# Graph attention in two layers: where each row's own logit terms lie, and which engine copies them out of PSUM

## The chip, the cores and the metric

The kernel runs on one core of a Trainium2 chip. A core has five engines that run beside each other[...]: PE (matrix products, which it writes to PSUM), DVE (vector operations), ACT (activations and copies), POOL (here it issues the indirect DMAs) and SP (here it issues the plain DMAs). Sixteen DMA engines move data between HBM and SBUF.

The metric is the device time in microseconds (us); the median of three runs counts. A time of this kernel is compared with another by that median. Inside one execution, the profile gives the start and length of every instruction.

## The reference

Eight graphs share one adjacency matrix of 2048 nodes (a node is its own neighbour too). Layer 0 is attention with one head on 256 features, layer 1 has four heads of 64. Cut to what matters:

```python
# layer 0: logits between node n and its neighbours m
e = leaky_relu((x @ W1) @ (x @ W2).T, 0.2)      # masked by adj
x = layernorm(x + relu(softmax(e) @ (x @ W3)))

# layer 1: four heads, D = 64
q = (x @ W).reshape(B, N, H, D)
e_src = einsum("bnhd,d->bnh", q, a[:D])          # a row's own term
e_dst = einsum("bnhd,d->bnh", q, a[D:])          # a neighbour's term
e = leaky_relu(e_src[:, :, None, :] + e_dst[:, None, :, :], 0.2)   # masked by adj
x = layernorm(x + elu(einsum("bijh,bjhd->bihd", softmax(e), q)))
```

Both terms are linear in x. So a row's q, its e_dst and its e_src come out of one product of x with a matrix of 256 + 4 + 4 columns. The neighbours need q and e_dst; only the row itself needs e_src.

## The kernel before

**Tiles and units.** The nodes are sorted by their number of neighbours and cut into 16 tiles of 128 rows (one row a partition). The eight graphs are two halves of four (HB = 4). A Unit is one layer, one half and one tile; there are 64, first the 32 of layer 0, then the 32 of layer 1. SLOTS gives each tile its number of neighbour slots, 12 to 38, 301 over all tiles.

**The ring.** For two slots at a time (CHUNK) POOL issues gathers of the neighbours' rows into one of 16 ring buffers (chunk_job, gather, L191). In layer 0 DVE multiplies each gathered row with the unit's vector g and sums it to a logit (logits0, L543), DVE and ACT make the softmax (L556 to L569), ACT weights the rows in place (sums0, L634), and PE sums them over the slots by products with an identity (add_slot, L612). Then the buffer is free for the next gather. In layer 1 DVE adds the own term to the gathered neighbour term (logits1, L747), most of the weighting is DVE's (L813), some of it ACT's (L809).

**The end of a unit of layer 0** is after0, and it is there that the change lies. The sum is transposed (L405, copied out of PSUM by ACT at L407), multiplied by W3 (projected, L415), added to the residual xr (L672), normalised (statistics, factors, normalise, L372 to L395) and stored to x1s (L687). Then y is transposed to x1T, and for each graph i of the half, with r, j = divmod(i, 2), two products of 264 columns (L696) go to one PSUM tile pq: 256 columns of q, 4 of e_dst, 4 of e_src. ACT copies the first 260 to qrow (L704); DVE copies the last 4 to the tile so (L705). Two DMAs on SP write so to the table own_d in HBM (L707, 32-byte pieces), and 8 steps later POOL scatters qrow to the table qg that layer 1 gathers from (store, L199).

qrow has one buffer, so two buffers, and the pool ps, from which pq comes, four banks for all products but the sums.

**Who reads own_d.** before1 loads the own terms of a unit of layer 1 as a whole row of 16 numbers (L728); logits1 adds them.

**What sets the order.** After the setup only POOL's order is the written one (manual_schedule with Pool). The instructions of PE, DVE, ACT and SP are put in an order for each engine when the program is built. In the code, tick advances at each slot the logits of coming units (stream), the starts of units (before0, before1), the end of the last unit (finish, after0) and the neighbour lists (neighbours, L491 to L500) by a step or two each. Every engine works through its own queue in order, so an instruction that waits holds all that stand behind it.

SP's queue carries in turn, for each unit of layer 0: four loads of xr (L512), the store of x1 (L687), the two stores of own terms (L707), later also the loads L728 and L787.

**The weights.** Weights.products computes the small columns: it multiplies W by a, and reduces over the 64 features of a head (L110) into wqs[:, k, 256:264].

Of the kernel before, what the change touches and what calls it, by code (L numbers as in the profile page):

```python
# [11 lines left out]
F32 = mybir.dt.float32  # L12
# [10 lines left out]
P = 128  # L23
ALPHA = 0.2
EPS = 1e-5
H = 4
# [21 lines left out]
class Weights:  # L48


    def __init__(self, nc, const, tmp, ps_tile, w1, w2, w3, wq, a, C, tag):
        KC = C // P
        self.ident = const.tile([P, P], F32, tag="ident", name=f"{tag}ident")
        make_identity(nc, self.ident)
        self.mhalf = const.tile([P, 1], F32, tag="mhalf", name=f"{tag}mhalf")
        nc.gpsimd.memset(self.mhalf, -0.5)
        self.roots = const.tile([P, 2], F32, tag="roots", name=f"{tag}roots")
        nc.gpsimd.memset(self.roots[:, 0:1], EPS)
        nc.gpsimd.memset(self.roots[:, 1:2], -math.log(2.0) / 3.0)
        self.w3 = const.tile([P, KC, C], F32, tag="w3", name=f"{tag}w3_sb")  # L60

        self.wqs = const.tile([P, KC, C + 2 * H], F32, tag="wqs", name=f"{tag}wqs")
        self.A = const.tile([P, KC, C], F32, tag="A", name=f"{tag}A")
        a_bc = const.tile([P, 2 * D], F32, tag="a_bc", name=f"{tag}a_bc")
        w12 = tmp.tile([P, 2, KC, C], F32, tag="t", name=f"{tag}w12")
        for t, src in ((w12[:, 0], w1), (w12[:, 1], w2), (self.w3, w3)):
            nc.scalar.dma_start(t, src.rearrange("(k p) d -> p k d", p=P))
        nc.scalar.dma_start(self.wqs[:, :, :C], wq.rearrange("(k p) d -> p k d", p=P))
        nc.scalar.dma_start(a_bc, a.rearrange("(o d) -> o d", o=1).to_broadcast([P, 2 * D]))

        self.given = w12, a_bc
        self.of = nc, tmp, ps_tile, C, tag

    def products(self):
        nc, tmp, ps_tile, C, tag = self.of
        w12, a_bc = self.given
        KC = C // P
        wT = tmp.tile([P, 2, KC, C], F32, tag="t", name=f"{tag}wT")

        for i in range(2):  # L80
            pt = ps_tile(f"{tag}ps_w{i}")
            ptv = pt[:, : KC * C].rearrange("p (k d) -> p k d", k=KC)
            for kd in range(KC):
                for kc in range(KC):
                    nc.tensor.transpose(
                        ptv[:, kd, ts(kc, P)], w12[:, i, kc, ts(kd, P)], self.ident
                    )
            nc.vector.tensor_copy(wT[:, i], ptv)
        pa = ps_tile(f"{tag}ps_A")
        for kc in range(KC):  # L90
            for kd in range(KC):
                nc.tensor.matmul(
                    pa[:, ts(kc, C)],
                    lhsT=wT[:, 0, kd, ts(kc, P)],
                    rhs=wT[:, 1, kd, :],
                    start=(kd == 0),
                    stop=(kd == KC - 1),
                )
        nc.vector.tensor_copy(self.A, pa[:, : KC * C].rearrange("p (k d) -> p k d", k=KC))

        for k in range(KC):
            for j in range(2):
                prod = tmp.tile([P, H, D], F32, tag="t", name=f"{tag}wa_{k}_{j}")
                nc.vector.tensor_tensor(
                    prod,
                    self.wqs[:, k, :C].rearrange("p (h d) -> p h d", h=H),
                    a_bc[:, ts(j, D)].unsqueeze(1).to_broadcast([P, H, D]),
                    ALU.mult,
                )
                nc.vector.tensor_reduce(  # L110
                    self.wqs[:, k, C + (1 - j) * H : C + (2 - j) * H], prod, AX.X, ALU.add
                )

    def rows_of(self, nc, const, j, C):

        self.wd = const.tile([P, C // P, P], F32, tag="wd", name="wd")
        nc.gpsimd.memset(self.wd, 0.0)
        for k in range(C // P):
            nc.vector.tensor_copy(
                self.wd[:, k, :].rearrange("p (h r) -> p h r", h=H)[:, :, 0],  # L120
                self.wqs[:, k, C + (1 - j) * H : C + (2 - j) * H],
            )
# [3 lines left out]
def fast_path(  # L126
# [24 lines left out]
    nc = tc.nc  # L151
    B, N, C = x.shape
    NT = N // P
    KC = C // P
    HB = B // 2
    HC = HB * C
    HG = HB * H
    HW = HC // 2
    CD = C + H
    QW = 2 * CD  # L160
# [3 lines left out]
    const = ctx.enter_context(tc.tile_pool(name="const", bufs=1))  # L164
# [5 lines left out]
    qp = ctx.enter_context(tc.tile_pool(name="q", bufs=1))  # L170
    hsp = ctx.enter_context(tc.tile_pool(name="hs", bufs=2))
    ep = ctx.enter_context(tc.tile_pool(name="e", bufs=3))
    sp = ctx.enter_context(tc.tile_pool(name="small", bufs=4))
# [9 lines left out]
    def ring_tile(name):  # L183
        return ring.tile([P, CHUNK * 2 * QW], F32, tag="ring", name=name)

    def wide_tile(name):
        return wp.tile([P, 2 * QW], F32, tag="t", name=name)
# [23 lines left out]
    own_d = [tc.dram_tile([N, HG], F32, name=f"own_{h}") for h in range(2)]  # L211
# [6 lines left out]
    w = Weights(nc, const, wp, ps_tile, w1, w2, w3, wq, a, C, "")  # L218
# [4 lines left out]
    for it in range(NT):  # L223
        r = ring_tile(f"adj_{it}")
# [99 lines left out]
    for r in range(2):  # L324
        rr = slice(64 * r, 64 * r + 64)
        pr = ps_tile(f"ps_half_{r}")[:, :NT]
        for c in range(2):
# [3 lines left out]
                rhs=ranked[rr, 0, :],  # L331
# [35 lines left out]
    def statistics(y, name):  # L367

        st = sp.tile([P, HB, nc.vector.BN_STATS_DIM], F32, tag="st", name=f"st_{name}", bufs=2)
        mv = sp.tile([P, HB, nc.vector.BN_AGGR_DIM], F32, tag="mv", name=f"mv_{name}")  # L370
        for b in range(HB):
            nc.vector.bn_stats(st[:, b, :], y[:, b, :])  # L372
            nc.vector.bn_aggr(mv[:, b, :], st[:, b, :])  # L373
            if b % 2 == 1:
                yield
        return mv
# [23 lines left out]
    def transposed(src, name, dst):  # L400

        for i in range(2):
            pt = ps_tile(f"ps_t_{name}_{i}")
            for j in range(4):
                nc.tensor.transpose(pt[:, ts(j, P)], src[:, ts(4 * i + j, P)], ident)  # L405
            yield
            nc.scalar.copy(dst[:, ts(i, 512)], pt)  # L407
        yield
# [253 lines left out]
    def after0(u):  # L662
        h, t, n = u.h, u.t, u.name
        while evictions:
            evictions.popleft()()
        hs = u.hs
        hT = wide_tile(f"hT_{n}")
        yield from transposed(hs, f"h_{n}", hT)
        y = wide_tile(f"y0_{n}")[:, :HC]

        def residual(i, pp):
            nc.vector.scalar_tensor_tensor(  # L672
                y[:, ts(i, 512)], pp, 0.0, u.xr[:, i, :], ALU.max, ALU.add
            )

        yield from projected(hT, w.w3, f"h_{n}", residual)
        yb = y.rearrange("p (b c) -> p b c", b=HB)
        mv = yield from statistics(yb, n)
        yield
        yield  # L680
        rstd, nmr = factors(mv, n)
        yield
        for b in range(HB):
            normalise(yb, yb, b, rstd, nmr)
            if b % 2 == 1:
                yield
        nc.sync.dma_start(x1s[h][ts(t, P), :], y)  # L687
        x1T = wide_tile(f"x1T_{n}")
        yield from transposed(y, f"x1_{n}", x1T)
        qrow = qp.tile([P, 2, QW], F32, tag="q", name=f"q_{n}")  # L690
        so = sp.tile([P, 2, HG // 2], F32, tag="so", name=f"so_{n}", bufs=2)
        for i in range(HB):
            r, j = divmod(i, 2)
            pq = ps_tile(f"ps_q_{n}_{i}")
            for k in range(KC):
                nc.tensor.matmul(  # L696
                    pq[:, : C + 2 * H],
                    lhsT=x1T[:, ts(i * KC + k, P)],
                    rhs=w.wqs[:, k, :],
                    start=(k == 0),  # L700
                    stop=(k == KC - 1),
                )
            yield
            nc.scalar.copy(qrow[:, r, ts(j, CD)], pq[:, :CD])  # L704
            nc.vector.tensor_copy(so[:, r, ts(j, H)], pq[:, CD : CD + H])  # L705
        for c in range(2):
            nc.sync.dma_start(  # L707
                own_d[h][ts(t, P), ts(c, HG // 2)].rearrange("(r p) g -> p r g", r=2),
                so[64 * c : 64 * c + 64],
            )  # L710

        def store():
            for r in range(2):
                scatter(
                    f"q{h}",
                    qg[h].rearrange("n (q c) -> (n q) c", q=2),
                    orderP[:, t, r : r + 1],
                    qrow[:, r, :],
                )
            tabled[0] += 1  # L720

        late.append((clock[0] + 8, store))


# [166 lines left out]
    for j, u in enumerate(units):  # L891
# [3 lines left out]
        elif j + 2 < NT:  # L895
            t = up[j + 2]
# [49 lines left out]
    for j, u in enumerate(units):  # L946
# [5 lines left out]
        if 2 <= j < 10:  # L952
            b, half = divmod(j - 2, 2)
            n = ts(half, N // 2)
# [311 lines left out]
```

## Time and profile before

| | |
|---|---|
| median of three runs | 2865.22 us (2856.55 to 2866.15) |
| the profiled execution | 2741.96 us, span from first to last instruction 2740.1 us |
| granted TensorE clock, mean | 0.842 |
| DMA | 749.51 MB, mean 274 GB/s |
| own-term stores (L707) | 64 issues of 4 KB, 1.8 us to landing, 615 ns of SP each |
| own-term copies (L705) | 128, first at 253.0 us, last at 1763.1 us |
| layer 0's logits (L543) | first at 136.6 us, last at 1683.4 us |
| layer 1's logits (L747) | first at 1686.3 us, last at 2687.6 us |

The span has three parts: the setup, whose last steps (the neighbour lists) run on beside layer 0; layer 0 until some 1780 us; and layer 1, which overlaps with the end of layer 0's last unit for some 100 us. In what follows a line of groups gives line, engine, operation, tiles and shapes, count | busy us and mean ns of one | the idle time of the engine just before them and what ended it. A line of waits gives who waited for whom, the sum in us, how often, and the longest. A line of the timeline gives the start in us, the length, the instruction and, in brackets, the idle time before it.

### The profile page before, as it was taken

What the parts mean: (1) busy time and instruction counts of PE and PEld (TensorE: products, weight loads), DVE (VectorE), ACT (ScalarE), POOL (GpSimd) and SP (SyncE); (2) the same over time, 40 slices, a digit from 0 to 9 for tenths busy, and PEclk for the clock granted to TensorE, in tenths of its full rate; (3) what the DMA queues carried; (4) which work ended last, traced back from release to release, by engine and by line L of the source; (5) the groups of instructions that cost most, each with busy time, mean ns of one, the idle gap of its engine ahead of it and who ended that gap; (6) DMA issues with size and microseconds to landing.
All of it is one profiled execution on the core that took longest, in us unless ns stands there. A gap on an engine that the chain in (4) does not pass through costs nothing. (4 is left out here: it accounts for less than half of the span.)

```text
span 2740.1 us, 42566 instructions
## 1 busy us (share of the span) xinstructions
PE 1857.8 (68%) x12003; PEld 792.3 (29%) x12003; DVE 2270.1 (83%) x7247; ACT 1827.9 (67%) x4937; POOL 1515.4 (55%) x1506
## 2 busy tenths in 40 slices
PE   0148888888786866686878767756656667655763
PEld 0124434333332333343434323312221222211221
DVE  7679999999987876777787786788888888888996
ACT  6137787878879986867878779644445555554454
POOL 1353454545444544544454545577767777777773
PEclk9569999999988988898988888877877878877876
DMA  9996776777765566767686774899789998997892
GB/s 388 380 376 207 270 262 245 260 245 263 261 221 200 183 215 215 252 212 268 219 277 217 242 263 154 287 332 357 268 315 354 348 344 317 358 351 269 305 354 89
DMA packets 248036, 749.51 MB, mean 274 GB/s; under 512 B 55712, under 2 KB 73248, under 8 KB 241648
## 3 DMA queue, kind: packets, MB, share of 16 engines
q0 software_dynamic: 192064, 644.32, 66.5%
q1 hardware_dynamic: 54464, 101.21, 10.4%
q8 instruction: 98, 1.61, 0.2%
q10 hardware_dynamic: 1264, 1.18, 0.1%
q14 instruction: 146, 1.20, 0.1%
HBM read 721.50 MB, written 84.48 MB: 294 GB/s over the span
## 5 line engine op out<-in xcount | busy, mean ns | idle before, releaser
L612 PE MATMUL acc<-s,ident 64*64 64x512 f32 x9632 | 1336.4, 653 | 469.0 <-issue 285.4
L543 DVE CUSTOM_DVE_ANT_0 j<-s,g 128x256 bf16<-128x256 f32 x2408 | 1019.9, 424 | 199.1 <-DMA s<-xg,idx 133.0
L191 POOL DMA_INDIRECT s<-xg,idx x602 | 632.4, 1051 | 771.7 <-ACT s L634 280.9
L634 ACT ACTIVATE s<-s,e 128x256 f32<-128x256 f32 x2408 | 1000.1, 506 | 28.3 <-DVE e L569 27.4
L191 POOL DMA_INDIRECT s<-qg,idx x602 | 614.8, 1021 | 233.4 <-issue 123.7
L612 PEld LDWEIGHTS acc<-s,ident 64*64 64x64 f32 x9632 | 391.1, 144 | 1211.5 <-issue 777.6
L813 DVE TENSOR_TENSOR s<-s,p 128x2048 f32<-128x2048 f32 (+1 forms) x262 | 577.5, 2222 | 0.0
L809 ACT ACTIVATE s<-s,e 128x64 f32<-128x64 f32 x1472 | 357.8, 335 | 47.1 <-DVE e L777 35.8
L543 DVE DVE_READ_ACCUMULATOR2_ANT e<- 128x1 f32 x2408 | 197.0, 82 | 0.0
L696 PE MATMUL ps_q<-wqs,x1T 128*128 128x264 f32 x512 | 147.7, 426 | 35.9 <-ACT x1T L407 25.1
L199 POOL DMA_INDIRECT out_dram<-o,oidx x128 | 130.2, 1017 | 71.5 <-ACT o L395 36.7
L405 PE MATMUL ps_t_x<-ident,xo 128*128 128x128 f32 x256 | 56.7, 365 | 162.7 <-DMA xo<-xg,order 162.6
L383 ACT ACTIVATE z<-mv,roots 128x4 f32<-128x4 f32 x64 | 19.0, 297 | 212.2 <-DVE mv L373 212.1
L747 DVE TENSOR_TENSOR e<-s,own 128x32 f32<-128x32 f32 (+1 forms) x312 | 56.9, 186 | 104.0 <-DMA s<-qg,idx 97.6
L415 PE MATMUL ps_p_g<-A,xT 128*128 128x256 f32 x512 | 129.4, 399 | 8.9 <-DVE so L705 5.2
L415 PE MATMUL ps_p_h<-w_sb,hT 128*128 128x256 f32 x512 | 127.8, 392 | 1.4 <-ACT hT L407 1.4
L696 PEld LDWEIGHTS ps_q<-wqs,x1T 128*128 128x128 f32 x512 | 100.8, 206 | 88.4 <-ACT x1T L407 32.8
L395 ACT ACTIVATE o<-xr,nmr,rstd 128x256 f32<-128x256 f32 x128 | 66.3, 589 | 76.9 <-DVE nmr L391 67.3
L415 PEld LDWEIGHTS ps_p_g<-A,xT 128*128 128x128 f32 x512 | 96.7, 196 | 53.2 <-ACT s L634 8.1
L763 ACT ACTIVATE e<-e 128x304 f32<-128x304 f32 (+11 forms) x34 | 14.9, 439 | 143.7 <-DVE e L762 143.7
L491 DVE MAX8 m<-nb 128x8 f32<-128x2048 f32 x44 | 100.5, 2286 | 11.9 <-DMA nb<-edges,order 11.7
L415 PEld LDWEIGHTS ps_p_h<-w_sb,hT 128*128 128x128 f32 x512 | 92.0, 189 | 63.3 <-issue 17.9
(130 smaller groups left out, 1486.2 us busy)
## 6 DMA issues: line engine op xcount, KB each, us to landing
adj<-in_adj_dram SPq DMA_DIRECT2D x16, 1024.0 KB, 8.9
edges<-adj SPq DMA_DIRECT2D x16, 1024.0 KB, 19.8
xr<-xo SPq DMA_DIRECT2D x128, 128.0 KB, 6.9
x1s<-y SPq DMA_DIRECT2D x32, 512.0 KB, 7.3
xr<-x1s SPq DMA_DIRECT2D x32, 512.0 KB, 6.9
s<-xg,idx POOLq DMA_INDIRECT x602
s<-qg,idx POOLq DMA_INDIRECT x602
xg<-in_x_dram SPq DMA_DIRECT2D x4, 2048.0 KB
```

The costliest lines, as they stand in the source:

```text
L191: nc.gpsimd.indirect_dma_start(out=dst, out_offset=None, in_=table, in_offset=AT(ap=index, axis=0), bounds_check=table.shape[0] - 1, oob_i ...
L199: ins = nc.gpsimd.indirect_dma_start(out=table, out_offset=AT(ap=index, axis=0), in_=src, in_offset=None)
L395: nc.scalar.activation(dst[:, b, :], y[:, b, :], AF.Identity, bias=nmr[:, b : b + 1], scale=rstd[:, b : b + 1],)
L415: nc.tensor.matmul(pp[:, ts(j, C)], lhsT=srcT[:, ts((2 * i + j) * KC + k, P)], rhs=weight[:, k, :], start=(k == 0), stop=(k == KC - 1),)
L491: nc.vector.max(m[:, ts(i, 8)], v)
L543: nc.vector.tensor_tensor_reduce(out=jt, in0=rows[:, s, ts(b, C)], in1=u.g[:, ts(b, C)], scale=1.0, scalar=0.0, op0=ALU.mult, op1=ALU.add, ...
L612: nc.tensor.matmul(acc[r][64 * c : 64 * c + 64, :], lhsT=ident[rr, rr], rhs=rows[rr, s, c * 2 * w_ : (c + 1) * 2 * w_].rearrange("p (j w) ...
L634: nc.scalar.activation(v, v, AF.Copy, scale=u.p[i][:, b, k : k + 1])
L696: nc.tensor.matmul(pq[:, : C + 2 * H], lhsT=x1T[:, ts(i * KC + k, P)], rhs=w.wqs[:, k, :], start=(k == 0), stop=(k == KC - 1),)
L747: nc.vector.tensor_tensor(e[:, c * CHUNK : c * CHUNK + ns, :].rearrange("p s (b g) -> p s b g", b=HB), rows[:, :ns, :].rearrange("p s (b w ...
L809: nc.scalar.activation(v[:, a, g, :], v[:, a, g, :], AF.Copy, scale=pv[:, a, g : g + 1])
L813: nc.vector.tensor_tensor(v, v, pv.unsqueeze(3).to_broadcast([P, n * HB, H, D]), ALU.mult)
```

## The change

The matrix of the small products gets four more columns, in front: sqs is [e_src | W | e_dst | e_src], and wqs is a view of its last 264 columns, so that all other users of wqs see what they saw. The four new columns are a copy of the last four.

For the first graph of a pair (j = 0) the product takes the columns from the front: own term, q, neighbour term. For the second (j = 1) it starts four columns later: q, neighbour term, own term. Side by side in qrow this gives own term, q, neighbour term, q, neighbour term, own term: the own terms lie at both ends, and what lies between is the table row of 520 numbers as before. ACT copies all 264 columns of pq, DVE none. The tile so is gone. The own terms are stored from qrow, by four DMAs of 16-byte pieces instead of two of 32-byte pieces, and the scatter takes the 520 numbers from between.

```diff
-        self.wqs = const.tile([P, KC, C + 2 * H], F32, tag="wqs", name=f"{tag}wqs")
+        self.sqs = const.tile([P, KC, C + 3 * H], F32, tag="wqs", name=f"{tag}wqs")
+        self.wqs = self.sqs[:, :, H:]
...
+            nc.vector.tensor_copy(self.sqs[:, k, :H], self.wqs[:, k, C + H :])
...
-        qrow = qp.tile([P, 2, QW], F32, tag="q", name=f"q_{n}")
-        so = sp.tile([P, 2, HG // 2], F32, tag="so", name=f"so_{n}", bufs=2)
+
+        qrow = qp.tile([P, 2, QW + 2 * H], F32, tag="q", name=f"q_{n}")
...
-                    rhs=w.wqs[:, k, :],
+                    rhs=w.sqs[:, k, j * H : j * H + CD + H],
...
-            nc.scalar.copy(qrow[:, r, ts(j, CD)], pq[:, :CD])
-            nc.vector.tensor_copy(so[:, r, ts(j, H)], pq[:, CD : CD + H])
+            nc.scalar.copy(qrow[:, r, ts(j, CD + H)], pq[:, : CD + H])
         for c in range(2):
-            nc.sync.dma_start(
-                own_d[h][ts(t, P), ts(c, HG // 2)].rearrange("(r p) g -> p r g", r=2),
-                so[64 * c : 64 * c + 64],
-            )
+            for j in range(2):
+                nc.sync.dma_start(
+                    own_d[h][ts(t, P), ts(2 * c + j, H)].rearrange("(r p) g -> p r g", r=2),
+                    qrow[64 * c : 64 * c + 64, :, j * (QW + H) : j * (QW + H) + H],
+                )
...
-                    qrow[:, r, :],
+                    qrow[:, r, H : H + QW],
```

Here C = 256, H = 4, CD = C + H = 260, QW = 2 * CD = 520, HG = 16.

## The prediction

> **What bounds the kernel now.** I read the page's busy shares and slices first, then the groups of the two instructions that the change touches.
>
> ```profile
> PE 1857.8 (68%) x12003; PEld 792.3 (29%) x12003; DVE 2270.1 (83%) x7247; ACT 1827.9 (67%) x4937; POOL 1515.4 (55%) x1506
> DVE  7679999999987876777787786788888888888996
> ACT  6137787878879986867878779644445555554454
> ...
> L704 ACT COPY q<-ps_q 128x260 f32<-128x260 f32 x128 | 47.0, 372 | 20.1 <-PE ps_q L696 20.1
> L705 DVE COPY so<-ps_q 128x4 f32<-128x4 f32 x128 | 20.0, 156 | 38.4 <-ACT q L704 38.3
> ```
>
> DVE is the busiest engine, but a slice is 68.5 us and the two layers differ, so I cut the span into stages. Columns are the stretch, its length, busy time of PE, PEld, DVE, ACT and POOL with counts, the granted clock, the DMA share and GB/s:
>
> ```profile
> 205.00:760.00 555.00, 462.99 (x2480) 210.27 (x2480) 533.84 (x2136) 434.41 (x1068) 261.30 (x249) 0.93 0.72 249
> 760.00:1780.00 1020.00, 764.37 (x4762) 355.88 (x4758) 776.99 (x3549) 822.31 (x2068) 491.20 (x472) 0.86 0.68 229
> 1780.00:2740.00 960.00, 583.45 (x4574) 199.25 (x4566) 816.92 (x1282) 492.45 (x1689) 692.02 (x677) 0.80 0.85 312
> ```
>
> Until about 760 us DVE is 96% busy (533.84 of 555): it is the bound there, because the neighbour lists are built on it beside the logits. From 760 to the end of layer 0 no engine is full. ACT leads with 81% (822.31 of 1020), and the work goes round a ring of 16 buffers: gather, DVE logits, ACT weighting, PE sum, next gather. From about 1780 layer 1 alone runs; the last copy of the changed line starts at 1763.1, so that part can only shift. The waits of 760 to 1715, DVE's and then ACT's (sum, count, longest):
>
> ```profile
> DVE j L543 <- DMA s<-xg,idx: 130.8, 86, 7.2
> DVE so L705 <- ACT q L704: 36.0, 24, 5.4
> ...
> ACT e L563 <- DVE e L562: 52.8, 17, 8.0
> ACT z L383 <- DVE mv L373: 29.8, 10, 8.1
> ACT s L634 <- DVE e L569: 12.5, 13, 1.6
> ACT y L395 <- DVE nmr L391: 11.1, 10, 3.2
> ```
>
> So the copy that moves matters by its wait, not its length. DVE stops for it 26 times in the run, 38.3 us, all after 760. The chain that ended last shows only the final scatters and decides nothing.
>
> The last view is DVE's instructions in order of time around a copy, one in the full stretch and one in the later stretch:
>
> ```profile
> 516.32 0.42 DVE L543 CUSTOM_DVE_ANT_0 j<-s,g 128x256 bf16<-128x256 f32 x1
> 516.66 0.09 DVE L543 DVE_READ_ACCUMULATOR2_ANT e<- 128x1 f32 x1
> 516.66 0.16 DVE L705 COPY so<-ps_q 128x4 f32<-128x4 f32 x1
> 516.78 0.42 DVE L543 CUSTOM_DVE_ANT_0 j<-s,g 128x256 bf16<-128x256 f32 x1
> 517.13 0.08 DVE L543 DVE_READ_ACCUMULATOR2_ANT e<- 128x1 f32 x1
> 517.25 0.42 DVE L543 CUSTOM_DVE_ANT_0 j<-s,g 128x256 bf16<-128x256 f32 x1
> ...
> 1303.93 0.16 DVE L705 COPY so<-ps_q 128x4 f32<-128x4 f32 x1 [1.49 <-ACT q L704]
> 1307.16 0.42 DVE L543 CUSTOM_DVE_ANT_0 j<-s,g 128x256 bf16<-128x256 f32 x1 [0.86 <-DMA s<-xg,idx]
> 1320.23 0.43 DVE L543 CUSTOM_DVE_ANT_0 j<-s,g 128x256 bf16<-128x256 f32 x1 [5.53 <-DMA s<-xg,idx]
> ```
>
> Two products with the copy between them start 0.46 us apart (516.32, 516.78); the next two, with none between, start 0.47 us apart (516.78, 517.25). The copy sits in the gap that the accumulator read leaves. And the 1.49 us lost at 1303.93 is followed by waits of 0.86 and 5.53 us for gathers.
>
> **What the Trainium skill says.** "PSUM — Partial Sum Buffer", section "PSUM bank collisions raise a hardware error": two engines must not touch one bank at once, two readers included, so they are ordered by semaphores. The trace agrees: the DVE copy starts after the ACT copy of the same bank, and 26 times DVE arrives early and waits. "VectorE: DVE Perf Modes", "The DRAIN you can't avoid": the next operation waits until the pipeline is empty, though one that is not held starts earlier. Here the measurement decides: the 0.16 us copy adds nothing between two products. "DMA: Bandwidth & Descriptors", "Specifications": transfers under 512 B are below line rate; this bears on the stores of 16 B pieces, of which the trace of before has only 32 B ones.
>
> **The change part by part.**
>
> *DVE copies removed.* 128 x 156 ns = 20.0 us of busy time. In the full stretch they ride in gaps as shown, so I count 0 to 2 us of path for the 45 copies before 760 (24 to 480, 21 to 760) and nothing for the later 83, since DVE has idle time there.
>
> *DVE's wait on ACT removed.* At most 38.3 us. What is late next, by place: at 1697.33 to 1705.33 four waits, 5.44 + 2.39 + 2.50 + 2.39 = 12.7 us, stand in the turn to layer 1, where ACT works through the last weights of layer 0 without a pause and the next exponential (1708.38) is queued behind them; worth 0. At 928.75 and 934.08, 4.7 us; ACT has no idle time from 915 to 965, so worth 0. The remaining 20.9 us are mostly followed within some 15 us by a gather wait of about the same or greater length, as at 1303.93; they pay only where DVE's lead reaches the end of a unit, where ACT waits for it. Upper reading of that: ACT waits for DVE 52.8 + 29.8 + 12.5 + 11.1 = 106.2 us from 760 to 1715; DVE itself waits 130.8 + 36.0 + 17.9 (its other five entries) = 184.7 us there, of which the copy's wait is 19.5%; 19.5% of 106.2 is 20.7 us. Lower reading: 3 us. I take the middle, 12 us.
>
> *PSUM banks freed by ACT's copy instead of DVE's.* PE waits for DVE's copy 5.7 us (L696) and 5.2 us (L415), before 760, where PE is 85% busy and DVE full. Between 0 and 10.9; I take 3.
>
> *ACT's copy grows from 260 to 264 columns.* 128x512 copies take 580 ns at L523 and 128x260 ones 372, so 208 / 252 = 0.83 ns a column; 4 columns x 128 copies = 0.4 us. On ACT, and hidden except where ACT is full.
>
> *Matmuls.* Still 264 columns (L696, 426 ns each), only from a window that starts 4 columns later for every second batch: 0.
>
> *SP's stores.* Four of 16 B pieces for each unit instead of two of 32 B: 64 more issues x 615 ns = 39 us of SP, 1.2 us a unit. What stands behind them on SP: the four residual loads (L512), then the x1 store (L687) and later own loads (L728). At 1013.23 the stores issue (1.28 us for two) and the next entry is at 1024.49, so two more delay nothing; and the loads are used a unit or more later. Without that cover it would be 1.2 x 32 = 38 us of lateness on SP. As to the DMA engines, the present stores land in 1.8 us (median); two times as many pieces I bound between 0 and 1 us of gather delay a unit, 0 to 32 us, and take 0, since the DMA share of layer 0 is 0.68 to 0.72 and the four are issued 0.6 us apart.
>
> *qrow's single buffer* is now read by these stores besides the two scatters. Before, it is free once the scatters land, about 20 us after the stores (stores 937.02, scatters 955.80 and 957.24), and the next unit's copies start at 1009.69, some 50 us later; the stores are not the last to let go. 0. Extra semaphore steps on ACT: 38 ns each, up to three a unit, 0 to 4 us; I take 0, in time ACT would have waited.
>
> *Setup.* Two DVE copies of 128x4, 0.3 us.
>
> *Order.* Only POOL's order is written out; the other queues are ordered when the program is built. In the code a q copy stands after one slot's four weightings, in the trace six of them stand between copies (931.01, 933.67), so the order is not the code's, and it may move with the DVE copies gone. Unseen; I bound it at 30 us either way and take 0.
>
> Sum: 12 + 3 - 0.3 = about 15 us. Against the profiled execution (2741.96 us, span 2740.1) this gives 2727. The runs' median, 2865.22, lies 4.5% above that execution, for which the page has no cause; I take the 15 us off unscaled: **2850 us**, -0.5%.
>
> **Rivals.**
> 1. *The wait is hidden anyway.* The gather waits take every freed microsecond: 3 us, 2862. For it: 1303.93, the two places where ACT is full, and the 130.8 us of gather waits beside 36.0. Against it: ACT does wait 106 us for DVE.
> 2. *The order turns against it* (slower). PE works in order and stands 132.5 us from 760 to 1715 at the transposes of xo (L405), 16 waits of 8.3 us each, because that gather lands late. While PE stands, no ring buffer is freed. If the new order puts those transposes about 1.5 us earlier against their gather in each of 32 units, that is 48 us, less the 15: 2898; it decides from 0.5 us a unit (16 us). A milder shift gives 2880. For it: the waits are long already and hang on the order alone. Against it: nothing in the change pushes them one way.
> 3. *The change doesn't do what it says*: DVE waits for ACT at another instruction (L566, L385) for the same reason. Same time as rival 1, and included there.
>
> **How the numbers follow.** About 0.5%, 14 us, is what a measurement can tell from no change. The forecast, with 15 us or more gained (2825 to 2851), 0.50; rivals 1 and 3, 0.25; rival 2, 0.25. A lucky order would carry the forecast to 2820. The range goes from 2818 to 2888, which leaves out the far end of rival 2 and an upper gain beyond 47 us. Faster 0.50, same 0.25, slower 0.25.
>
> **What would show it.** Right: no L705, DVE's gather waits grow by less than 25 us, ACT's waits on DVE fall below 90 us, PE's waits on so vanish, layer 0 ends some 15 us sooner and layer 1 keeps its length. Rival 1: gather waits up by 30 us or more. Rival 2: PE's wait on xo well above 162.6 us in total. The forecast fails if layer 1 changes its length by more than layer 0 does, or if ACT begins to wait for DMAs before its copy.

## The result, and the profile after

The changed kernel takes 2857.53 us (median of 20 runs, 2847.68 to 2862.42), the kernel before 2864.71 us on the same chip (20 runs). The ratio is 0.9975, with a 95% interval from 0.9967 to 0.9984: 7 us faster, between 5 and 10. The direction is the one forecast; the gain is just under half of the 15 us.

A warning ahead of all comparisons: the profiled execution after takes 2856.72 us, that of before took 2741.96. The change did not add 115 us. By all signs the two were taken on chips of different speed (the last section), so traces of after are compared here with an execution of the unchanged kernel on a chip where it takes 2865.09 us.

The page after, busy shares and DVE's slices; then the copy in the view of groups:

```profile
PE 2098.3 (73%) x12003; PEld 913.0 (32%) x12003; DVE 2268.4 (79%) x7121; ACT 1837.8 (64%) x4937; POOL 1511.6 (53%) x1506
DVE  7678999998988876777886866787777778877886
```

```profile
L706 ACT COPY q<-ps_q 128x264 f32<-128x264 f32 x128 | 47.5, 373 | 13.7 <-PE ps_q L698 13.5 <-PE ps_p_g L417 0.2
```

The first slices of DVE are as full as before (9 from slice 5 on); the later ones are lower, because layer 1 does the same work in more time on this chip. DVE has 126 instructions fewer (7247 to 7121: 128 copies gone, two in the setup added), and ACT's copy is as long as before (373 ns against 372). Code lines below L62 have moved down by one or two, so L543 is L545 now, and L704 is L706. The stages:

```profile
205.00:760.00 555.00, 454.68 (x2414) 208.65 (x2416) 517.48 (x2019) 427.86 (x1052) 253.41 (x242) 0.91 0.71 243
760.00:1780.00 1020.00, 776.20 (x4643) 359.79 (x4637) 769.94 (x3503) 818.38 (x2044) 484.39 (x465) 0.86 0.68 227
```

DVE is still the fullest engine until 760 us (517.48 of 555), ACT from then on. The waits of 760 to 1715, first DVE's, then ACT's:

```profile
DVE j L545 <- DMA s<-xg,idx: 129.3, 76, 6.9
DVE j L545 <- DVE e L545: 17.4, 29, 1.0
```

```profile
ACT e L565 <- DVE e L564: 57.3, 14, 11.5
ACT z L385 <- DVE mv L375: 16.4, 6, 7.7
ACT s L636 <- DVE e L571: 8.8, 9, 1.4
```

DVE's wait on ACT's copy is gone. In the unchanged kernel on a chip of this speed the same window shows:

```profile
DVE j L543 <- DMA s<-xg,idx: 112.4, 66, 7.3
DVE so L705 <- ACT q L704: 22.7, 20, 2.9
```

So 22.7 us of one wait went, and the gather wait grew by 16.9 (129.3 against 112.4). That already looks more like the first rival than like the forecast. Layer 1 kept its length: its logits run from 1701.9 to 2802.3 us after, from 1708.8 to 2811.1 in the unchanged kernel on the chip of that speed. Both are some 1101 us, so in these two traces most of the gain, 6.9 us, lies in layer 0. Of that, only 2.3 us had come when the 900th of DVE's 2408 products with gathered rows started (counted in the traces: 752.2 us against 754.5); the rest came later.

### The profile page after: what moved, and what is told of

Read it like the earlier page. It is cut to its first block, busy times and chain, and to the rows that moved or that the text cites. A ratio compares the mean times of both kernels' runs of the same rounds, so it can differ in the third digit from the quotient of the medians.

```text
span 2854.9 us, 42520 instructions
## 1 busy us (share of the span) xinstructions
PE 2098.3 (73%) x12003; PEld 913.0 (32%) x12003; DVE 2268.4 (79%) x7121; ACT 1837.8 (64%) x4937; POOL 1511.6 (53%) x1506
## 4 chain that ended last, share of the span: by engine, by line
PE 28%; DVE 23%; issue 19%; DMA 14%; ACT 8%; POOL 6%; another core or an unknown queue 1%; POOLq 0%; DVEq 0%; ACTq 0%; SPq 0%
PE acc L614 21%; DVE j L545 11%; ACT s L636 6%; DMA s<-xg,idx 4%; POOL s L193 4%; DMA xo<-xg,order 4%; DMA s<-qg,idx 3%; DVE s L815 2%; DVE m L493 2%; PE ps_p_g L417 2%; PE ps_p_h L417 2%; DVE e L545 2%; PE ps_q L698 1%; PE ps_t_x L407 1%
## 5 line engine op out<-in xcount | busy, mean ns | idle before, releaser
L614 PE MATMUL acc<-s,ident 64*64 64x512 f32 x9632 | 1572.3, 667 | 352.1 <-issue 209.7
L545 DVE CUSTOM_DVE_ANT_0 j<-s,g 128x256 bf16<-128x256 f32 x2408 | 1019.7, 423 | 239.7 <-DMA s<-xg,idx 129.8
L614 PEld LDWEIGHTS acc<-s,ident 64*64 64x64 f32 x9632 | 507.4, 146 | 1210.2 <-issue 941.5
L811 ACT ACTIVATE s<-s,e 128x64 f32<-128x64 f32 x1472 | 364.0, 336 | 82.7 <-issue 35.3
L545 DVE DVE_READ_ACCUMULATOR2_ANT e<- 128x1 f32 x2408 | 196.0, 81 | 0.0
L407 PE MATMUL ps_t_x<-ident,xo 128*128 128x128 f32 x256 | 56.3, 362 | 138.9 <-DMA xo<-xg,order 132.1
L493 DVE MAX8 m<-nb 128x8 f32<-128x2048 f32 x44 | 100.4, 2284 | 10.4 <-DMA nb<-edges,order 10.3
```

Of the source, the lines that this page charges most:

```text
L493: nc.vector.max(m[:, ts(i, 8)], v)
L545: nc.vector.tensor_tensor_reduce(out=jt, in0=rows[:, s, ts(b, C)], in1=u.g[:, ts(b, C)], scale=1.0, scalar=0.0, op0=ALU.mult, op1=ALU.add, ...
L614: nc.tensor.matmul(acc[r][64 * c : 64 * c + 64, :], lhsT=ident[rr, rr], rhs=rows[rr, s, c * 2 * w_ : (c + 1) * 2 * w_].rearrange("p (j w) ...
L811: nc.scalar.activation(v[:, a, g, :], v[:, a, g, :], AF.Copy, scale=pv[:, a, g : g + 1])
```

## The experiments

Three batches were run, each on one chip, and each kernel is compared with the kernel before on that chip. Where a kernel copies something that nothing uses, this is said.

### First batch: is it the wait or the bank?

**The kernel before, unchanged.**

> The kernel before, unchanged, for a profile whose span is near the median of its runs (the profiled execution of before was 4.3% shorter than that) and for the noise. Every theory expects a ratio of 1.000 within 0.001. If the profile is again near 2740 us, the profiled execution is what differs; near 2860, the layer 1 part is the one that is longer.

Measured: 2865.59 us, ratio 1.0004 (0.9994 to 1.0013). This is what no change looks like, and its trace is the reference above.

**The wait put back, without the bank.** DVE copies the own terms out of qrow once ACT has written them. The copy is unused. DVE waits for ACT as before, but PSUM is read by ACT alone.

```diff
             nc.scalar.copy(qrow[:, r, ts(j, CD + H)], pq[:, : CD + H])
+            own = j * (CD + H) + j * CD
+            nc.vector.tensor_copy(so[:, r, ts(j, H)], qrow[:, r, own : own + H])
```

> The changed kernel, with one addition: DVE copies the four own terms from qrow (SBUF) to a tile that nothing reads, so that DVE again waits for ACT's copy, but holds no PSUM bank. Waits theory (the 7 us gained are DVE's waits on ACT that are gone): they come back, ratio to before 0.999 to 1.001, DVE waits on ACT for this copy some 30 us in all. Banks theory (the gain is PSUM banks given back sooner by ACT): ratio stays 0.997 to 0.998.

Measured: 2855.35 us, ratio 0.9971 (0.9960 to 0.9982). DVE's waits from 760 to 1715 in this kernel:

```profile
DVE j L545 <- DMA s<-xg,idx: 116.4, 63, 7.1
DVE so L709 <- ACT q L707: 29.0, 22, 4.2
```

The wait is back in full (29.0 us, against 22.7 in the unchanged kernel), the gather wait is down again, and the whole gain is still there. The wait was worth nothing that these runs can tell.

**Wait and bank put back.** DVE copies the same four columns straight from the PSUM tile. The copy is unused.

```diff
             nc.scalar.copy(qrow[:, r, ts(j, CD + H)], pq[:, : CD + H])
+            nc.vector.tensor_copy(so[:, r, ts(j, H)], pq[:, j * CD : j * CD + H])
```

> The changed kernel, with one addition: DVE copies the four own terms from the PSUM tile to a tile that nothing reads, so that both the wait and the hold on the bank are back; what is left of the change are the wider copy, the stores of 16 B pieces and the longer rows. Waits theory and banks theory: ratio to before 0.999 to 1.001. A theory that the four stores or the longer rows cost something which the rest of the change outweighs: 1.002 or more.

Measured: 2860.93 us, ratio 0.9990 (0.9979 to 1.0001). By the medians, more than half of the gain is gone.

**The copies without wait or bank, free to be placed.** DVE copies a small tile (nmr) in SBUF that has long been ready. The copy is unused.

```diff
             nc.scalar.copy(qrow[:, r, ts(j, CD + H)], pq[:, : CD + H])
+            nc.vector.tensor_copy(so[:, r, ts(j, H)], nmr)
```

> The changed kernel, with one addition: 128 DVE copies of 128x4 from a tile that DVE itself made some time before (nmr), so the copies are back and no wait on ACT is. Waits and banks theories: the copies ride in gaps, ratio to before 0.997 to 0.998 as for the change. Copies theory (DVE's 20 us of busy time are what was gained): 0.999 to 1.001.

Measured: 2865.16 us, ratio 1.0002 (0.9992 to 1.0013). No theory had this. But the program had put these copies elsewhere: in pairs behind the small operations of the normalisation, ahead of where the others lie. So the next batch holds them in place.

### Second batch: the copy's place, the stores, and DVE's slack

**The same copies at the old places.** An edge that orders, but makes nothing wait, keeps each behind ACT's copy in the planned order.

```diff
-            nc.scalar.copy(qrow[:, r, ts(j, CD + H)], pq[:, : CD + H])
+            one = nc.scalar.copy(qrow[:, r, ts(j, CD + H)], pq[:, : CD + H])
+            two = nc.vector.tensor_copy(so[:, r, ts(j, H)], nmr)
+            tc.add_manual_dep(two.ins, one.ins.name, ..., reason="order alone")
```

> The changed kernel, with 128 DVE copies of 128x4 from nmr (made by DVE long before), put one by one where the old copies stood by an order-only edge, without a wait on ACT and without a hold on PSUM; the order of all engines is that of wait_back but for some 30 DVE and 12 ACT places. Banks theory (the gain is the PSUM banks that PE gets back sooner): ratio to before 0.997 to 0.998, as wait_back; then copy_free lost its gain by where its copies stand (in pairs behind nmr). Copies theory (DVE's copies cost what was gained): 0.999 to 1.001, and wait_back stays unexplained.

Measured: 2737.5 us, ratio 0.9975 (0.9966 to 0.9985). At their old places 128 copies cost nothing.

**The kernel before, with ACT making the small copy.** Here no engine but ACT reads the bank, in two instructions.

```diff
-            nc.vector.tensor_copy(so[:, r, ts(j, H)], pq[:, CD : CD + H])
+            nc.scalar.copy(so[:, r, ts(j, H)], pq[:, CD : CD + H])
```

> The kernel before, with the 128x4 copy to the tile so made by ACT as an instruction of its own right behind the copy of 260 columns; DVE copies nothing, two stores of 32 B pieces as before. Banks theory: most of the gain is here too, less some 25 us of ACT time in layer 0 that is mostly hidden: 0.997 to 0.999. Copies theory and waits theory: 0.997 to 0.998 as well. A theory that the gain comes from the wider single copy or the stores: 1.000 or more.

Measured: 2745.25 us, ratio 1.0007 (0.9998 to 1.0016): nothing gained. The group of the new copies:

```profile
L705 ACT COPY so<-ps_q 128x4 f32<-128x4 f32 x128 | 22.5, 176 | 0.0
```

DVE is out of the bank, and ACT has 22.5 us more to do. The two could cancel, but the traces don't show that. DVE's products in this kernel, in the one with the copies from SBUF at the old places, and in the one with four stores (next), where DVE copies from the bank; the line gives ns (least, median, most), then the first and the last start:

```profile
L543 DVE CUSTOM_DVE_ANT_0 j<-s,g x2408: 391/424/499, 136.8 to 1676.4; 128x256 bf16<-128x256 f32 x186
L545 DVE CUSTOM_DVE_ANT_0 j<-s,g x2408: 392/424/503, 135.7 to 1677.1; 128x256 bf16<-128x256 f32 x186
L543 DVE CUSTOM_DVE_ANT_0 j<-s,g x2408: 390/424/500, 136.1 to 1687.5; 128x256 bf16<-128x256 f32 x186
```

With ACT's extra copies layer 0 is as short as in the kernel that gains. The gain is lost after it: from the first to the last, layer 1's logits take 1008.0 us, against 1005.3 and 1000.7. These are single executions, and the one of this kernel is the quickest of its 13. Why nothing is gained in all stays open.

**The kernel before, with four stores.** Everything else is as before.

```diff
-            nc.sync.dma_start(
-                own_d[h][ts(t, P), ts(c, HG // 2)].rearrange("(r p) g -> p r g", r=2),
-                so[64 * c : 64 * c + 64],
-            )
+            for j in range(2):
+                nc.sync.dma_start(
+                    own_d[h][ts(t, P), ts(2 * c + j, H)].rearrange("(r p) g -> p r g", r=2),
+                    so[64 * c : 64 * c + 64, :, ts(j, H)],
+                )
```

> The kernel before, with the own terms stored by four DMAs of 16 B pieces instead of two of 32 B, all else and the order of every other instruction the same. All theories of mine: the stores are hidden, 0.999 to 1.001. If the stores give back part of the gain: 1.001 to 1.004.

Measured: 2743.05 us, ratio 0.9999 (0.9989 to 1.0009). The smaller pieces cost nothing.

**Work added to DVE where it waits for gathers.** The changed kernel, with 64 operations of 128x512 on DVE behind the q copies of the second half of layer 0, their result unused.

```diff
+            if h == 1:
+                two = nc.vector.scalar_tensor_tensor(
+                    pad, wa, nmr[:, i : i + 1], wa, ALU.mult, ALU.add
+                )
```

> The changed kernel, with a DVE operation of 128x512 (about 0.6 us more of DVE time, result unused) at each of the 64 places of the old copies in the second half of layer 0, some 38 us of DVE in all, about as much as the waits that the change removed; no wait on ACT. If gather waits take up what DVE gains or loses there (my account of why the removed waits gave nothing): less than 8 us longer than the changed kernel, ratio to before 0.997 to 1.000. If DVE's time counts there: 1.008 to 1.011.

Measured: 2737.62 us, ratio 0.9975 (0.9965 to 0.9985), the same ratio as the changed kernel and as the copies at the old places. Each operation took 747 ns (median; the expectation had 0.6 us), so 64 x 0.747 = 48 us of DVE went in from 1044 us on, and cost nothing that can be told from zero. DVE's wait for gathers from 760 to 1715, with the small copies at the old places and with the added work:

```profile
DVE j L545 <- DMA s<-xg,idx: 152.4, 93, 7.0
DVE j L545 <- DMA s<-xg,idx: 121.8, 82, 6.7
```

The gather wait gives up 30.6 us to the added work.

### Third batch: repeats on one chip, and DVE's slack in the first half

The code of the first three is that of the kernels above.

**Copies from SBUF at the old places, again.**

> The changed kernel with the 128 DVE copies of 128x4 added at their old places, read from SBUF, their result unused; a repeat beside the next two, so that the three stand on one chip. Banks theory (the gain comes from PSUM banks that DVE no longer holds): ratio to before 0.997 to 0.998, as 0.9975 before. If the 0.9975 was the chip's or chance: 0.999 to 1.001.

Measured: 2838.51 us, ratio 0.9968 (0.9956 to 0.9981).

**Copies from the PSUM bank, again.**

> The same copies read from the PSUM bank (result unused), so that DVE waits for ACT and holds the bank again. Banks theory: 0.999 to 1.0005, and at least 0.0012 above the kernel that reads SBUF, on the same chip; DVE ends waits of PE at the projection and at the q products before 760 us, some 8 to 13 us. If banks are worth nothing: the same ratio as the kernel that reads SBUF within 0.001.

Measured: 2842.28 us, ratio 0.9986 (0.9975 to 0.9997). That is 0.0018 above its neighbour, as on the first chip (0.9990 against 0.9971, or 0.0019). The ratio itself missed its lower bound of 0.999 by a little. PE's waits on DVE's copy from 205 to 985 us, all of them before 760:

```profile
PE ps_p_g L417 <- DVE so L708: 8.3, 3, 3.0
PE ps_q L699 <- DVE so L708: 3.9, 4, 3.1
```

12.2 us, as expected. In the kernel that copies from SBUF there is none of these; there PE waits 6.1 us for ACT's copy at the q products. One of these waits in the timeline of the kernel with the copies from PSUM (weight loads, accumulator reads and POOL are left out):

```profile
607.04 0.65 ACT L707 COPY q<-ps_q 128x264 f32<-128x264 f32 x2
607.38 0.41 DVE L545 CUSTOM_DVE_ANT_0 j<-s,g 128x256 bf16<-128x256 f32 x1
607.73 2.29 DVE L493 MAX8 m<-nb 128x8 f32<-128x2048 f32 x1
607.98 1.05 PE L699 MATMUL ps_q<-wqs,x1T 128*128 128x264 f32 x4
608.96 1.09 PE L614 MATMUL acc<-s,ident 64*64 64x512 f32 x8
609.93 0.40 DVE L545 CUSTOM_DVE_ANT_0 j<-s,g 128x256 bf16<-128x256 f32 x1
...
610.34 2.27 DVE L496 MATCH_REPLACE8 nb<-m,nb 128x2048 f32<-128x2048 f32 x1
612.53 0.41 DVE L545 CUSTOM_DVE_ANT_0 j<-s,g 128x256 bf16<-128x256 f32 x1
612.87 0.15 DVE L708 COPY so<-ps_q 128x4 f32<-128x4 f32 x1
...
613.08 1.95 PE L417 MATMUL ps_p_g<-A,xT 128*128 128x256 f32 x4 [3.03 <-DVE so L708]
```

Read it from the copies. ACT is done with the banks at 607.7. DVE's first 0.15 us copy starts at 612.87, more than 5 us later. It is not waiting: DVE never stops, but two operations of 2.3 us that build the neighbour lists (MAX8 and MATCH_REPLACE8) and three products stand ahead of it. Until it is done the bank isn't free, and PE, which needs one for the next g, stands 3.03 us. Over the first half of layer 0 the copies from PSUM of this kernel end 1.63 us after ACT's on average (64 banks, 104 us; worked out from the starts and lengths in the trace). What this costs in the end the trace can't show: it is of the quickest of this kernel's 22 executions (2832.56 us), quicker than that of its neighbour (2837.73).

**Copies from SBUF, free to be placed, again.**

> The same copies read from SBUF and free to be placed: in pairs right behind the normalisation's small operations (result unused). If the 1.0002 of the first time is real: 1.000 again, 0.002 above the kernel with the copies at the old places, and the place of instructions in DVE's queue is worth as much as the whole gain. If it was chance: 0.997 to 0.998.

Measured: 2844.25 us, ratio 0.9994 (0.9978 to 1.0009): 0.0026 above the kernel with the copies at the old places. The loss has come twice now, so it is hardly chance. Its cause is open. The copies themselves are not longer (163 ns, median, against 165 at the old places), and PE's queue has the same order. DVE's and ACT's have not: compared in the built programs, 66 of DVE's 7080 other instructions and 43 of ACT's 4791 stand elsewhere than with the copies at the old places. Behind the copies the view of waits has only 2.2 us of new waits in the first half (6.4 us in the run of the first batch).

**Work added to DVE in the first half of layer 0.** As in the second batch, with h == 0 for h == 1.

> The changed kernel with 64 DVE operations of 128x512 added (result unused), some 0.6 us each, 38 us in sum, behind the q copies of the first half of layer 0, where DVE is full until about 760 us. If DVE's own time is the bound there: ratio to before 1.005 to 1.011, layer 0's last logit 20 to 35 us later. If DVE has slack there too: 0.997 to 0.999, as with the same operations in the second half (0.9975).

Measured: 2870.79 us, ratio 1.0087 (1.0071 to 1.0103). Against the kernel with the copies at the old places on this chip (2838.51) that is 32 us for the 48 us that went in:

```profile
L710 DVE SCALAR_TENSOR_TENSOR pad<-A,nmr 128x512 f32<-128x512 f32 x64 | 47.8, 747 | 0.0
```

In the traces, PE's sums that end at 770.0 us with the copies at the old places end 36.1 us later with the added work, and DVE's last product of layer 0 starts 32.4 us later (1723.3 against 1690.9 us; 20 to 35 were expected). So all of it is lost before 770 us: DVE's time counts there and is free in the second half. (The added work also moves some 150 of PE's products in its queue, so DVE's time is not all that differs.)

## Why the forecast had the direction and not the size

**Shown, the step that failed: "DVE's wait on ACT removed", 12 us.** It was the largest term, the middle between a lower reading of 3 us and an upper one of 20.7. Measured it is nothing that can be told from zero: the kernel with 29.0 us of that wait put back has 0.9971, the changed one 0.9975, and the one with such copies at the old places and no wait 0.9975 and 0.9968. Of these, the kernel with the wait and the last one have nearly the same order in every queue (compared in the built programs, 36 of DVE's other 7080 instructions and 13 of ACT's 4791 stand elsewhere). The upper reading took the copy's share of DVE's waits (19.5%) as its share of ACT's waits for DVE. That needs DVE's lost time to reach ACT, and DVE has slack in that stretch: 48 us of added work there cost nothing. The first rival had this step right, for the reason given there: the gather wait takes what the other wait gives up. Its 3 us for the whole change were too few, though (5 to 10 measured). Without the 12 us the forecast's own sum is 2.7 us, so that it came within a factor of some two of the gain was luck as far as this term goes.

**Not shown: where the 7 us come from, and what "PSUM banks freed by ACT's copy instead of DVE's", 3 us, is worth.** PE's waits for DVE's copy are there (12.2 us in the trace of the third batch, against 6.1 for ACT's copy in its neighbour). The page of the Trainium skill quoted ahead, "PSUM — Partial Sum Buffer", section "PSUM bank collisions raise a hardware error", says that engines on one bank must be ordered. The forecast priced this order first of all as DVE's wait for ACT. The trace shows a third party: PE waits for the second reader, and the second reader stands in the queue of the engine that is full.

On two chips the kernels in which DVE reads the bank are 0.0019 and 0.0018 slower than those in which DVE's copy reads SBUF at about the same place: 0.0019 x 2865.09 = 5.4 us, 0.0018 x 2847.38 = 5.1 us (the medians as they stand differ by 5.6 and 3.8). With the intervals of the four ratios combined, the mean difference is 0.0018 with about 0.0011 either way, so 2 to 8 us. If that were the price of the held bank, it would be inside the bounds given (0 to 10.9) and above the value taken.

But the hold is not all that differs. Compared in the built programs, the kernel with the copies from PSUM has PE's and DVE's queues in exactly the order of the kernel before. In the kernel with the copies from SBUF at the old places, 7 of PE's 6392 products, 262 of DVE's 7080 and 123 of ACT's 4791 stand elsewhere (7, 265 and 120 in the one with the wait put back). Order is thus a full rival to the bank. It need not cost anything: the changed kernel differs from the one with the copies at the old places in 211 of DVE's and 74 of ACT's, at the same ratio. But it can be dear: the pairs of copies placed early hold no bank and wait for nobody, and lose 9.8 and 5.7 us against the same neighbours (medians). In the traces both losses lie in the same stretch, where DVE is full. In the first batch DVE's 900th product starts at 748.6 us with the wait put back, 9.8 us later with the copies from PSUM and 6.0 us later with the early pairs. In the third it starts at 744.4 us with the copies at the old places, and 4.9 and 5.5 us later. A kernel that holds the bank in the order of the changed one was not run, so hold and order are not parted.

Two more observations do not fit a bank that explains all. PE's waits on DVE's copies lie before 760 us (all but 4.4 us of them in the trace that has most after it), but most of the gain of the traces comes later: 2.3 of 6.7 us before the 900th product in the result's traces, 2.5 of 10.4 between the four stores and the copies at the old places. And the kernel that has the wait, the hold and the order of before keeps part of the gain (0.9990, and 0.9986 with an interval that ends at 0.9997). What it has of the change is the wide copy and the stores from qrow, of which four stores alone gave nothing (0.9999).

**Shown at the price taken.** The copies, 0: put back at the old places, they leave 0.9975 and 0.9968. The four stores, 0: 0.9999. ACT's wider copy: 373 ns against 372. Layer 1: the same length. PE's waits on so are gone, as forecast. One reading was a little off: PE is 85% busy only until 480 us; for the stage up to 760 the line shown gives 83% (462.99 of 555). And the prediction took 0.5% as the least that a measurement can tell; the 20 runs of each kernel tell 0.1%.

**Signs that came out.** "Gather waits grow by less than 25 us" came true (16.9), and so did "ACT's waits on DVE below 90 us" (57.3 + 16.4 + 8.8, and 1.1 for y on nmr, make 83.6). Neither says anything for the wait theory. The same four pairs sum to 82.1 us in the unchanged kernel on the chip of that speed (38.8 + 25.4 + 13.0 + 4.9), and its gather wait differs by 18.4 us between two chips (130.8 and 112.4). Rival 1's own sign, gather waits up by 30 us or more, did not come, although its reason held. Such signs need a kernel before from the same chip.

**The slower rival, a planner's order that turns against the change, did not come.** PE's wait on the transposes of xo is 132.1 us after and 129.2 in the unchanged kernel on the chip of that speed; it named "well above 162.6". That an order can cost 0.2% is not refuted: the two runs with early pairs suggest it.

**The median above the profiled execution** was left without a cause, and the 15 us were taken off unscaled. The chips explain the gap, and ratios carry over between them: the copies at the old places give 0.9975 where the kernel before takes 2743.77 us, and 0.9968 where it takes 2847.38.

## What to carry to other kernels

Where two engines read one PSUM bank, ask when the second of them gets to it: if its queue is full of long operations, a copy of 0.15 us holds the bank for microseconds, and PE can be the one that waits. A wait counts at its engine's slack, not at its length: put the wait back alone, or add dummy work in the same stretch, before believing in it. Where the order of the queues is made when the program is built, taking small instructions away can move hundreds of others (270 of DVE's here). A difference of 0.2% belongs to the mechanism that one has in mind only when the order is the same on both sides.

## What the runs showed of the hardware that was not expected

The same program takes different times on different chips: the kernel before has medians of 2743.77, 2847.38 and 2865.09 us on the chips of the three batches, each with all its runs within 0.5% of its median. Most of the difference is layer 1: its logits span 1001 us in the profile shown before (1686.3 to 2687.6) and 1102 us in the unchanged kernel on the slowest of the three (1708.8 to 2811.1). From 1780 to 2740 us the trace moves 312 GB/s in the one and 294 in the other, while the granted clock is not lower on the slow chip (0.84 against 0.80). On the slow chip DVE also stands up to 1.0 us between two products with nothing in the trace that ends the wait:

```profile
DVE j L543 <- DVE e L543: 16.4, 31, 1.0
```

This line is of the unchanged kernel there, 760 to 1715 us; the profile shown before the change has no such entry. Why chips differ was not tried. It is a reason to compare kernels only on one chip, and not to subtract a profile's time from a median of other chips.
